# A Mamba block between two ternary feed-forward layers: the convolution reads u from PSUM

## The chip, the cores and the metric

One core of a Trainium2 chip. The metric is the device time of one execution in microseconds; lower is better. PE is TensorE, DVE VectorE, ACT ScalarE, POOL GpSimd, and SP the engine whose queue issues most DMAs.

## What is computed

For x of 4096 rows and 1024 columns, all in float32:

```python
x = x + 0.5 * ffn(layernorm(x))      # weight 1024x1024 made ternary: clip(round(w / mean|w|)) * mean|w|, and a bias
x = x + mamba(layernorm(x))
x = x + 0.5 * ffn(layernorm(x))      # the same weight and bias

def mamba(x):                        # 1024 channels, 16 states a channel
    u, z = split(x @ W_in.T)
    u = silu(conv_b + sum(conv_w[:, k] * up[:, k:k+L] for k in range(4)))   # up: u with three rows of zeros in front
    dt_r, B, C = split(u @ W_xproj.T)                                       # 64, 16, 16 columns
    dt = softplus(dt_r @ W_dt.T + b_dt)
    h_t = exp(dt_t * A) * h_(t-1) + dt_t * B_t * u_t                        # for each channel and state
    y = sum over states of (h_t * C_t) + u * Dskip
    return (y * silu(z)) @ W_out.T
```

The convolution is along the sequence: each row needs the three rows in front of it.

## The kernel before

The sequence is cut into 16 chunks of T = 256 rows. u, dt and the states h lie with the channels on the partitions and time along the free dimension; x, z and y lie with time on the partitions. u of a chunk is eight blocks of 128 channels, four to a half.

**Stages of a chunk.** `front()`: the first feed-forward layer (`ffn`: statistics on ACT and POOL, normed rows on ACT at L412, transposes on PE at L428, a split into a high and a low part at L456 and L458, matmuls at L499, the residual on DVE at L479), a second normalisation with its transposes, of which ACT makes the tile xT (L599), and then u: eight blocks of eight matmuls, each of which moves 256 columns of xT (L628). A float32 matmul appears in the profile as two passes. After each block a stream `conv` is spawned. `gates()` makes z (L680, L694, L699). `steps()` makes B, C and dt (L645 to L725). The recurrence runs state by state for each half: ACT makes the decays (L916), POOL the inputs dt*u*B (L937), DVE scans (L969) and multiplies by C (L984), some products are added in pairs on DVE (L999), and PE transposes and sums them in PSUM (L1022). `back()`: the gate (L1039), transposes (L755), W_out (L763), the residual on DVE (L734), the last feed-forward layer, and the output.

**The convolution before.** Two blocks share one PSUM bank: block j of a pair lies in columns j*256 and on. `conv` copies the last three columns of the chunk in front from the tile halo into the tile up (POOL, L556), copies the block from PSUM into up (ACT, L558), has POOL copy up's last three columns to halo for the next chunk (L548), makes the bias and the newest tap from PSUM (ACT, L561), and adds the three older taps one after the other on DVE, both tensor inputs in SBUF (L573):

```python
end = yield act(T, at)
nc.scalar.copy(up[:, KER - 1 :], rows_)
...
    nc.vector.scalar_tensor_tensor(ub, up[:, k : k + T], tap, ub, ALU.mult, ALU.add)
```

The bank is given back once ACT has read the pair's second block. After four blocks ACT applies silu to the half (L580).

**What sets the order.** The instructions of each engine run in the order in which they are issued, and a planner written into the kernel (the class `Streams`) chooses that order while the program is built. Each stage is a generator, a stream, with a rank; before an instruction it yields the engine, an assumed duration, the earliest time, and whether it needs the port that DVE and POOL share. The planner always issues the instruction that can start first by these assumptions, ties by rank; `HOLD` lets an engine wait some time for a stream of better rank. Constants are assumed costs and delays: `REACH` from one engine to another, `ISSUE` and `ADDED` for the DMA that adds the bias to x (L472, issued by POOL), `LATE_*` extra delays, and `DECAY`, `ENTER`, ..., `FFN_C`, `Z` the ranks. All of this only sets the order; on the chip semaphores decide when each instruction starts.

**Buffers.** PSUM has eight banks: three in the pool `banks` (u, z, out, feed-forward, transposes and dt take turns there), three for the decays, two for y. SBUF has five weight tiles of 512 KB, shared by the tiles of W_in for u, those for z, and those of W_out; `streamed()` keeps up to `ahead` tiles of one kind asked for. SP issues these loads (L364 u, L371 z, L377 W_out), and between them 512 broadcasts of B and C from DRAM (L886), x and the output.

Of the kernel before, what the change touches and what calls it, by code (L numbers as in the profile page):

```python
# [35 lines left out]
ALU = mybir.AluOpType  # L36
# [5 lines left out]
NST = 16  # L42
RANK = 64
KER = 4
EPS_LN = 1e-5
EPS_W = 1e-10

# [3 lines left out]

FULL, PASS, TURN = 0.844, 0.455, 0.855
REACH = 160
ISSUE, ADDED = 950, 9000
SWITCH = 1300

LATE_P, LATE_D, LATE_E, LATE_N = 300, 300, 300, 300
PAIRED = range(0, 4, 2)

DECAY, ENTER, SUM, PREPARE, RECUR, GATE = 4, 2, 1, 0, 5, 4  # L60
FFN_A, NORM, U_PART, CONV, DELTA, OUT, FFN_C = 0, 2, 3, 1, 0, 2, 3

HOLD = 100, 0, 250, 100
Z = 1, 4


class Streams:
# [109 lines left out]
def macaron_mamba_kernel(  # L177
# [34 lines left out]
    decays = buffers(3, [P, 2, T], "da", pool_=psum)  # L212
    ys = buffers(TT, [P, OH], "y", pool_=psum)
    xs = buffers(7, [P, D], "x")
    xts = buffers(2, [P, NB, T], "xT")
    his = buffers(2, [P, NB, P], "hi", F32R)
    los = buffers(2, [P, NB, P], "lo", F32R)
    weights = buffers(5, [P, D], "weight")
# [1 line left out]
    szs = buffers(2, [P, TT, OH], "sz")  # L220
    dts = buffers(2, [P, HB, T], "dt")
    tmps = buffers(2, [P, D], "tmp")
    ups = buffers(3, [P, KER - 1 + T], "up")
    xds = buffers(2, [P, 2, T], "xd")
    lns = buffers(4, [P, 40], "ln")
    hs = buffers(3, [P, HB, T], "h")
# [215 lines left out]
    def ffn(c, which, rank, at, tiles=range(TT)):  # L442
        ln, rows_, at = yield from stats(c, at, tiles)
        key = which, c

        def split(t):

            xn, begin = yield from normed(c, ln, rows_, t, at)
            hi = yield from his.take()
            lo = yield from los.take()  # L450
            ends = []

            def cut(g, pt, at_):
                part_hi, part_lo = (flat(p_[:, 4 * g : 4 * g + 4, :]) for p_ in (hi, lo))
                end = yield act(512, at_)
                nc.scalar.copy(part_hi, pt)  # L456
                end = yield dve(640, end + REACH)
                nc.vector.tensor_tensor(part_lo, pt, part_hi, ALU.subtract)  # L458
                banks.put(pt, end)
                ends.append(end)  # L460
                if len(ends) == NB // 4:
                    ready["parts", key, t] = end + REACH + LATE_N
                    parts[t] = lo, hi

            order.spawn(biased(t, begin), rank)
            yield from transposed(xn, begin, cut, rank)

        def biased(t, at_):

            yield from when("hbias")  # L470
            end = yield pool(ISSUE, at_, False)
            nc.gpsimd.dma_start(x_tiles[c, t], hbias.to_broadcast([P, D]), accum_op=ALU.add)  # L472
            ready["bias", key, t] = end + ADDED

        def residual(t, cols, pf, at_):
            at_ = max(at_, (yield from when("bias", key, t)))
            end = yield dve(650, at_)
            xt = x_tiles[c, t][:, cols]
            nc.vector.scalar_tensor_tensor(xt, pf, hscl, xt, ALU.mult, ALU.add)  # L479
            (ys if (*key, t) == ("a", 0, 1) else banks).put(pf, end)  # L480
            ready["ffn", key, t, cols.start] = end
            if key == ("c", NC - 1):
                yield from give_out(c, t, cols, end)

        parts = {}
        for t in tiles:
            order.spawn(split(t), rank)
        if key == ("a", 0):
            yield from as_weights_come(key, parts, residual, rank)
        for t in tiles if key != ("a", 0) else ():  # L490
            begin = yield from when("parts", key, t)
            lo, hi = parts[t]
            for h in range(2):
                cols = slice(h * OH, (h + 1) * OH)
                pf = yield from banks.take()
                for x in (lo, hi):
                    end = yield pe(8 * OH * PASS, 0, "r")
                    for k in range(NB):
                        nc.tensor.matmul(  # L499
                            pf,  # L500
                            x[:, k, :],
                            wf[:, k, cols],
                            start=(x is lo and k == 0),
                            stop=(x is hi and k == NB - 1),
                        )
                order.spawn(residual(t, cols, pf, end + REACH), rank)
            los.put(lo, end)
            his.put(hi, end)
        lns.put(ln, end if key != ("a", 0) else order.now)
        ends = {}  # L510
        for t in tiles:
            left = yield from when("ffn", key, t, 0)
            right = yield from when("ffn", key, t, OH)
            ends[t] = max(left, right)
        return ends
# [27 lines left out]
    u, sz, dt, xd, bc_dram, over = {}, {}, {}, {}, {}, {}  # L543


    def hand_over(c, blk, up, at):
        end = yield pool(140, at)
        nc.gpsimd.tensor_copy(halo[:, blk, :], up[:, T:])  # L548
        ready["halo", c, blk] = end

    def conv(c, blk, pp, at):
        half, b = divmod(blk, HB)
        up = yield from ups.take()
        ub, rows_ = u[c, half][:, b, :], pp[:, blk % 2, :]
        yield pool(140)
        nc.gpsimd.tensor_copy(up[:, 0 : KER - 1], halo[:, blk, :])  # L556
        end = yield act(T, at)
        nc.scalar.copy(up[:, KER - 1 :], rows_)  # L558
        order.spawn(hand_over(c, blk, up, end + REACH), CONV)
        end = yield act(T)  # L560
        nc.scalar.activation(  # L561
            ub,
            rows_,
            AF.Identity,
            bias=pr[:, blk, C_CB : C_CB + 1],
            scale=pr[:, blk, C_CW + KER - 1 : C_CW + KER],
        )
        if blk % 2:
            banks.put(flat(pp), end)
        for k in range(KER - 1):  # L570
            end = yield dve(405, end + (REACH if k == 0 else 115), True)
            tap = pr[:, blk, C_CW + k : C_CW + k + 1]
            nc.vector.scalar_tensor_tensor(ub, up[:, k : k + T], tap, ub, ALU.mult, ALU.add)  # L573
        end = max(end, (yield from when("halo", c, blk)))
        ups.put(up, end)
        done = ready.setdefault(("conv", c, half), [])
        done.append(end)
        if len(done) == HB:
            end = yield act(D, end + REACH, "silu")
            nc.scalar.activation(flat(u[c, half]), flat(u[c, half]), AF.Silu)  # L580
            ready["u", c, half] = end + REACH

    def front():
        for c in range(NC):
# [5 lines left out]
                at[t] = order.now + 5000  # L590
            ends = yield from ffn(c, "a", FFN_A, at)
            yield NORM
            queue = streamed(u_weights, NB, 2, U_PART)
            ln, rows_, at = yield from stats(c, ends)
            xT = yield from xts.take()

            def keep(g, pt, at_):
                end = yield act(512, at_)
                nc.scalar.copy(  # L599
                    xT[:, 4 * g : 4 * g + 4, t * P : (t + 1) * P],  # L600
                    pt.rearrange("p (j q) -> p j q", q=P),
                )
                banks.put(pt, end)
# [7 lines left out]
            for t in range(TT):  # L611
                xn, at = xns[t]
                yield from transposed(xn, at, keep, NORM)
                while len(ends) < 2 * (t + 1):
                    yield lambda: ends[2 * t + 1] if len(ends) > 2 * t + 1 else INF
            yield U_PART
            for pair in range(NB // 2):
                if 2 * pair % HB == 0:
                    u[c, 2 * pair // HB] = yield from us.take()
                pp = yield from banks.take()  # L620
                pp = pp.rearrange("p (j t) -> p j t", t=T)
                for j in range(2):
                    w = yield from arrived(queue)
                    wt = w.rearrange("p (k m) -> p k m", m=P)
                    for k in range(NB):
                        if k % 4 == 0:
                            end = yield pe(8 * T * FULL)
                        nc.tensor.matmul(  # L628
                            pp[:, j, :], wt[:, k, :], xT[:, k, :], start=(k == 0), stop=(k == NB - 1)
                        )  # L630
                    order.spawn(conv(c, 2 * pair + j, pp, end + REACH), CONV)
                    weights.put(w, end)
            order.spawn(gates(c, xT), Z[0])
            order.spawn(steps(c), DELTA)

# [26 lines left out]
        xds.put(xd[c], order.now + 2000)  # L662

    def gates(c, xT):
        queue = streamed(z_weights, NB, 3, Z[0])
        for half in range(2):
            yield Z[half]
            sz[c, half] = yield from szs.take()
            for b in range(0, HB, 2):
                pp = yield from banks.take()  # L670
                pp = pp.rearrange("p (t j) -> p t j", t=TT)
                for part_ in range(2):
                    w = yield from arrived(queue)
                    wt = w.rearrange("p (j k m) -> p j k m", j=2, m=P)
                    for t in range(TT):
                        end = yield pe(8 * T * FULL)
                        for i in range(HB):
# [1 line left out]

                            nc.tensor.matmul(  # L680
                                pp[:, t, :],
                                xT[:, k, t * P : (t + 1) * P],
                                wt[:, :, i, :],
                                start=(k == 0 and t == 0),
                                stop=(k == NB - 1),
# [91 lines left out]
    def back():  # L777
        for c in range(NC - 1):
            yield OUT
            queue = streamed(lambda i, w: out_weights(i // 2, i % 2, w), NB, 2, OUT)  # L780
            yT = []
            for half in range(2):
                yT.append((yield from us.take()))
                yield from turned(c, half, yT[half])
            for q in range(D // QW):
# [6 lines left out]
                        by_w_out(po, yT[half], w, half, t)  # L792
                    weights.put(w, end)
                for t in range(TT):
                    order.spawn(mixed(c, q, t, po, end + REACH), OUT)
            for half in range(2):
                us.put(yT[half], end)
            for q in range(D // QW):
# [324 lines left out]
```

## Time and profile before

| | |
|---|---|
| median of 3 runs | 2696.09 us (2694.91 to 2696.83) |
| the profiled execution | 2698.07 us, of which the span of the instructions is 2696.3 |
| granted TensorE clock, mean | 0.977 |
| HBM | 151 GB/s over the span |
| chain that ended last, shares | PE 35%, DVE 27%, ACT 15%, issue 12% |

The profile is of one execution. A group of instructions is named by its line, its engine, its operation and its tiles (out<-in); "busy" is the union of its instructions' times and "mean ns" the mean of one. Idle time ahead of a group is put down to the instruction whose semaphore came last. PE's ends are modelled: a pass of 256 columns is shown as 379 ns, while the next starts 216 ns after it. PEld is the load of the weights, which lies beside the matmuls.

### The profile page before, as it was taken

The page shows a single profiled execution, that of the slowest core. Times are in us where ns is not written, and L with a number is a line of the kernel's source. Part 1 is how long each engine was busy: PE and PEld are TensorE (multiplying, and loading weights), DVE is VectorE, ACT ScalarE, POOL GpSimd, SP SyncE. Part 2 cuts the span into 40 slices and gives each one's busy share as a digit, 9 for nine tenths or more (in the row PEclk, how much of TensorE's full clock was granted, in tenths as well). Part 3 has the DMA queues.
Part 4 walks back from the last instruction along what each step waited for, and adds up shares of the span by engine and source line. Part 5 has one row for each costly group of instructions (what it writes and reads, how often), then busy time and mean ns, then how long its engine had stood idle before and what let it go on. Part 6 is the DMA issues. An engine that isn't in the chain of part 4 may idle for free.

```text
span 2696.3 us, 40026 instructions
## 1 busy us (share of the span) xinstructions
PE 2522.3 (94%) x13570; PEld 2150.7 (80%) x13570; DVE 2436.7 (90%) x2500; ACT 2012.7 (75%) x4214; POOL 1802.3 (67%) x1657
## 2 busy tenths in 40 slices
PE   5988899999999999999999999999999999999887
PEld 4776788888888888888888888888888888888676
DVE  4588999999998999989999998999999899999894
ACT  3678688696877869687786878879687786967663
POOL 0356767677676776767677675767767577676773
PEclk8998899999999999999999999999999999999888
DMA  5443445645544555545555644554554456445451
GB/s 164 140 153 99 134 144 168 180 145 164 168 144 147 164 180 153 157 154 153 160 157 162 183 145 131 174 173 143 172 169 145 136 176 182 144 161 149 129 152 40
DMA packets 218550, 410.77 MB, mean 152 GB/s; under 512 B 19172, under 2 KB 85860, under 8 KB 218344
## 3 DMA queue, kind: packets, MB, share of 16 engines
q1 hardware_dynamic: 209128, 374.65, 42.3%
q0 software_dynamic: 9216, 33.56, 6.8%
q8 instruction: 107, 1.75, 0.3%
q14 instruction: 99, 0.81, 0.1%
HBM read 390.82 MB, written 17.31 MB: 151 GB/s over the span
## 4 chain that ended last, share of the span: by engine, by line
PE 35%; DVE 27%; ACT 15%; issue 12%; POOL 2%; DMA 2%; DVEq 0%; SPq 0%; POOLq 0%; ACTq 0%
DVE h L969 14%; PE bank L628 11%; DVE p L984 9%; PE bank L499 7%; PE bank L680 6%; ACT da L916 4%; PE y L1022 4%; PE bank L645 2%; PE bank L763 2%; DVE p L999 2%; PE bank L428 2%; ACT u L561 1%; DVE x L734 1%; POOL h L937 1%; ACT L916 1%
## 5 line engine op out<-in xcount | busy, mean ns | idle before, releaser
L937 POOL TENSOR_TENSOR h<-u,bc 128x1024 f32<-128x1024 f32 x512 | 1226.2, 2395 | 517.7 <-ACT da L916 212.0
L969 DVE TENSOR_TENSOR_SCAN h<-da,h 128x512 f32<-128x512 f32 x1024 | 1212.0, 1205 | 53.9 <-ACT da L916 42.2
L916 ACT ACTIVATE da<-dt,pr 128x255 f32<-128x255 f32 x2048 | 945.9, 474 | 89.2 <-DVE h L969 59.1
L984 DVE TENSOR_TENSOR p<-h,bc 128x1024 f32<-128x1024 f32 x512 | 684.8, 1338 | 0.1
L1022 PE MATMUL y<-ident,p 128*128 128x128 f32 x3840 | 513.5, 279 | 72.9 <-DVE p L984 65.0
L1022 PEld LDWEIGHTS y<-ident,p 128*128 128x128 f32 x3840 | 450.1, 144 | 139.7 <-DVE p L984 92.1
L628 PE MATMUL bank<-xT,weight 128*128 128x256 f32 x2048 | 472.8, 384 | 43.7 <-ACT u L561 32.2
L680 PE MATMUL bank<-weight,xT 128*128 128x256 f32 x2048 | 478.0, 381 | 0.0
L628 PEld LDWEIGHTS bank<-xT,weight 128*128 128x128 f32 x2048 | 380.5, 191 | 114.9 <-ACT u L561 53.4
L763 PE MATMUL bank<-weight,u 128*128 128x256 f32 x2016 | 465.4, 380 | 0.1
L680 PEld LDWEIGHTS bank<-weight,xT 128*128 128x128 f32 x2048 | 378.4, 191 | 46.1 <-issue 1.0
L763 PEld LDWEIGHTS bank<-weight,u 128*128 128x128 f32 x2016 | 371.5, 191 | 46.4 <-ACT da L916 1.8
L944 POOL TENSOR_TENSOR h<-h,over 128x4 f32<-128x4 f32 x512 | 285.4, 557 | 27.6 <-issue 0.3
L952 ACT COPY state<-h 128x4 f32<-128x4 f32 x512 | 98.8, 193 | 270.4 <-DVE h L969 269.7
L573 DVE SCALAR_TENSOR_TENSOR u<-up,pr,u 128x256 f32<-128x256 f32 x384 | 214.5, 591 | 95.4 <-ACT u L561 92.4
L499 PE MATMUL bank<-wf,lo 128*128 128x512 f32 x976 | 255.9, 404 | 4.2 <-DVE lo L458 3.7
L499 PE MATMUL bank<-wf,hi 128*128 128x512 f32 x976 | 247.5, 396 | 0.0
L499 PEld LDWEIGHTS bank<-wf,lo 128*128 128x128 f32 x976 | 180.6, 190 | 47.3 <-DVE lo L458 5.4
L499 PEld LDWEIGHTS bank<-wf,hi 128*128 128x128 f32 x976 | 182.5, 189 | 38.4
L548 POOL COPY halo<-up 128x3 f32<-128x3 f32 x128 | 45.7, 357 | 165.1 <-ACT up L558 164.9
L428 PE MATMUL bank<-ident,tmp 128*128 128x128 f32 x756 | 116.0, 285 | 32.0 <-ACT tmp L412 21.9
L558 ACT COPY up<-bank 128x256 f32<-128x256 f32 x128 | 47.0, 367 | 121.5 <-PE bank L628 119.1
(99 smaller groups left out, 2232.5 us busy)
## 6 DMA issues: line engine op xcount, KB each, us to landing
bc<-bcd SPq DMA_DIRECT2D x512, 256.0 KB, 3.7
weight<-in_w_out SPq DMA_DIRECT2D x128, 512.0 KB, 4.8
weight<-in_w_in SPq DMA_DIRECT2D x128, 512.0 KB, 3.7
weight<-in_w_in SPq DMA_DIRECT2D x256, 256.0 KB, 5.9
x<-hbias POOLq DMA_DIRECT2D x64, 512.0 KB, 8.2
x<-in_x SPq DMA_DIRECT2D x32, 512.0 KB, 5.2
out<-x SPq DMA_DIRECT2D x30, 512.0 KB, 4.5
weight<-in_w_ffn SPq DMA_DIRECT2D x5, 512.0 KB, 7.4
```

What stands on the lines that cost most here:

```text
L428: nc.tensor.matmul(pt[:, j * P : (j + 1) * P], xn[:, k * P : (k + 1) * P], ident, start=(j == 0), stop=(j == 3), is_transpose=True, skip_g ...
L499: nc.tensor.matmul(pf, x[:, k, :], wf[:, k, cols], start=(x is lo and k == 0), stop=(x is hi and k == NB - 1),)
L573: nc.vector.scalar_tensor_tensor(ub, up[:, k : k + T], tap, ub, ALU.mult, ALU.add)
L628: nc.tensor.matmul(pp[:, j, :], wt[:, k, :], xT[:, k, :], start=(k == 0), stop=(k == NB - 1))
L680: nc.tensor.matmul(pp[:, t, :], xT[:, k, t * P : (t + 1) * P], wt[:, :, i, :], start=(k == 0 and t == 0), stop=(k == NB - 1), skip_group_c ...
L763: nc.tensor.matmul(po[:, t, :], yT[:, b, t * P : (t + 1) * P], wt[:, b, :], start=(half == 0 and t == 0 and b == 0), stop=(half == 1 and b ...
L916: nc.scalar.activation(da[:, i, 1:], dt[c, half][:, b, 1:], AF.Exp, scale=a_neg[:, half * HB + b, n : n + 1],)
L937: nc.gpsimd.tensor_tensor(h, u[c, half], bc[:, 0:1, :].to_broadcast([P, HB, T]), ALU.mult)
L944: nc.gpsimd.tensor_tensor(h[:, :, 0], h[:, :, 0], over[c, half][:, :, n], ALU.add)
L969: nc.vector.tensor_tensor_scan(rows_, flat(da), rows_, 0.0, ALU.mult, ALU.add)
L984: nc.vector.tensor_tensor(p, h, bc[:, 1:2, :].to_broadcast([P, HB, T]), ALU.mult)
L1022: nc.tensor.matmul(y[t][:, b * P : (b + 1) * P], p[:, b, t * P : (t + 1) * P], ident, start=(first and b == 0), stop=(n == NST - 1 and b = ...
```

## The change

The convolution reads u where the matmuls leave it. A block now has a bank of its own, and its matmuls move 259 columns: the three of the chunk in front, whose u is computed a second time, and the 256 of this one. For that xT has four more columns in front (`PAD`), and halo holds three columns of xT instead of u: POOL copies them in ahead of a chunk's u matmuls and saves the new ones after the first block, two copies a chunk instead of sixteen. The tile up, ACT's copy into it, and the POOL copies for each block are gone. The taps on DVE have one input in PSUM, are reckoned at 335 instead of 405 ns, and are no longer planned as users of the shared port. The bank is given back after the third tap.

W_out's tiles are asked for once the product of state 12 of a chunk's second half is there, up to three ahead (before: at the chunk's start of `back()`, up to two). u's tiles are asked for up to four ahead (two), z's two (three). The residuals of the feed-forward layers and of W_out are planned 300 ns later (`LATE_X`), the bias DMA at 6000 instead of 9000 ns, and most ranks and one `HOLD` have other values.

```diff
-ISSUE, ADDED = 950, 9000
+ISSUE, ADDED = 950, 6000
-LATE_P, LATE_D, LATE_E, LATE_N = 300, 300, 300, 300
+LATE_P, LATE_X, LATE_D, LATE_E, LATE_N = 300, 300, 300, 300, 300
-DECAY, ENTER, SUM, PREPARE, RECUR, GATE = 4, 2, 1, 0, 5, 4
-FFN_A, NORM, U_PART, CONV, DELTA, OUT, FFN_C = 0, 2, 3, 1, 0, 2, 3
-HOLD = 100, 0, 250, 100
-Z = 1, 4
+DECAY, ENTER, SUM, PREPARE, RECUR, GATE = 5, 3, 1, 0, 5, 1
+FFN_A, NORM, U_PART, CONV, DELTA, OUT, FFN_C = 1, 0, 3, 2, 2, 2, 3
+HOLD = 100, 0, 250, 500
+Z = 2, 4
-    xts = buffers(2, [P, NB, T], "xT")
+    xts = buffers(2, [P, NB, PAD + T], "xT")
-    ups = buffers(3, [P, KER - 1 + T], "up")
...
     def conv(c, blk, pp, at):
         half, b = divmod(blk, HB)
-        up = yield from ups.take()
-        ub, rows_ = u[c, half][:, b, :], pp[:, blk % 2, :]
-        yield pool(140)
-        nc.gpsimd.tensor_copy(up[:, 0 : KER - 1], halo[:, blk, :])
+        ub, rows_ = u[c, half][:, b, :], pp[:, KER - 1 : KER - 1 + T]
         end = yield act(T, at)
-        nc.scalar.copy(up[:, KER - 1 :], rows_)
-        order.spawn(hand_over(c, blk, up, end + REACH), CONV)
-        end = yield act(T)
         nc.scalar.activation(
...
-        if blk % 2:
-            banks.put(flat(pp), end)
         for k in range(KER - 1):
-            end = yield dve(405, end + (REACH if k == 0 else 115), True)
+            end = yield dve(335, end + (REACH if k == 0 else 95))
             tap = pr[:, blk, C_CW + k : C_CW + k + 1]
-            nc.vector.scalar_tensor_tensor(ub, up[:, k : k + T], tap, ub, ALU.mult, ALU.add)
-        end = max(end, (yield from when("halo", c, blk)))
-        ups.put(up, end)
+            nc.vector.scalar_tensor_tensor(ub, pp[:, k : k + T], tap, ub, ALU.mult, ALU.add)
+        banks.put(pp, end)
...
-            queue = streamed(u_weights, NB, 2, U_PART)
+            queue = streamed(u_weights, NB, 4, U_PART)
...
+            end = yield pool(190)
+            nc.gpsimd.tensor_copy(xT[:, :, PAD - KER + 1 : PAD], halo)
+            at = max(end, ends[-1]) + REACH
             yield U_PART
-            for pair in range(NB // 2):
...
+            for blk in range(NB):
...
+                    nc.tensor.matmul(
+                        pp[:, : KER - 1 + T],
+                        wt[:, k, :],
+                        xT[:, k, PAD - KER + 1 : PAD + T],
+                        start=(k == 0),
+                        stop=(k == NB - 1),
+                    )
+                order.spawn(conv(c, blk, pp, end + REACH), CONV)
+                weights.put(w, end)
+                if blk == 0:
+                    yield pool(190, at)
+                    nc.gpsimd.tensor_copy(halo, xT[:, :, PAD + T - KER + 1 : PAD + T])
...
-        queue = streamed(z_weights, NB, 3, Z[0])
+        queue = streamed(z_weights, NB, 2, Z[0])
...
         for c in range(NC - 1):
             yield OUT
-            queue = streamed(lambda i, w: out_weights(i // 2, i % 2, w), NB, 2, OUT)
             yT = []
             for half in range(2):
+                if half:
+                    yield from when("product", c, 1, 12)
+                    queue = streamed(lambda i, w: out_weights(i // 2, i % 2, w), NB, 3, OUT)
```

In the changed kernel the lines of the parts spoken of are L550 (ACT's read of u), L560 (taps), L604 and L627 (POOL's two copies), L616 (u matmuls); the recurrence's and the later lines stand three to five lines further up than before (L966 scans, L981 products, L996 pair sums, L1019 y).

More of the change, by code (lines that the diff above doesn't have):

```diff
@@ L44 @@
 KER = 4
+PAD = 4
 EPS_LN = 1e-5
@@ L505, in ffn @@
                         )
-                order.spawn(residual(t, cols, pf, end + REACH), rank)
+                order.spawn(residual(t, cols, pf, end + REACH + LATE_X), rank)
             los.put(lo, end)
@@ L543, in macaron_mamba_kernel @@
     u, sz, dt, xd, bc_dram, over = {}, {}, {}, {}, {}, {}
[L546 to L549, printed above, removed]
     def conv(c, blk, pp, at):
         half, b = divmod(blk, HB)
-        up = yield from ups.take()
-        ub, rows_ = u[c, half][:, b, :], pp[:, blk % 2, :]
-        yield pool(140)
-        nc.gpsimd.tensor_copy(up[:, 0 : KER - 1], halo[:, blk, :])
+        ub, rows_ = u[c, half][:, b, :], pp[:, KER - 1 : KER - 1 + T]
         end = yield act(T, at)
-        nc.scalar.copy(up[:, KER - 1 :], rows_)
-        order.spawn(hand_over(c, blk, up, end + REACH), CONV)
-        end = yield act(T)
         nc.scalar.activation(
@@ L599, in keep @@
                 nc.scalar.copy(
-                    xT[:, 4 * g : 4 * g + 4, t * P : (t + 1) * P],
+                    xT[:, 4 * g : 4 * g + 4, PAD + t * P : PAD + (t + 1) * P],
                     pt.rearrange("p (j q) -> p j q", q=P),
@@ L615, in front @@
                     yield lambda: ends[2 * t + 1] if len(ends) > 2 * t + 1 else INF
+            end = yield pool(190)
+            nc.gpsimd.tensor_copy(xT[:, :, PAD - KER + 1 : PAD], halo)
+            at = max(end, ends[-1]) + REACH
             yield U_PART
-            for pair in range(NB // 2):
-                if 2 * pair % HB == 0:
-                    u[c, 2 * pair // HB] = yield from us.take()
+            for blk in range(NB):
+                if blk % HB == 0:
+                    u[c, blk // HB] = yield from us.take()
                 pp = yield from banks.take()
[L621 to L632, printed above, removed]
+                w = yield from arrived(queue)
+                wt = w.rearrange("p (k m) -> p k m", m=P)
+                for k in range(NB):
+                    if k % 4 == 0:
+                        end = yield pe(8 * (KER - 1 + T) * FULL, at)
+                    nc.tensor.matmul(
[10 more added lines that the diff above has]
+                    nc.gpsimd.tensor_copy(halo, xT[:, :, PAD + T - KER + 1 : PAD + T])
             order.spawn(gates(c, xT), Z[0])
@@ L681, in gates @@
                                 pp[:, t, :],
-                                xT[:, k, t * P : (t + 1) * P],
+                                xT[:, k, PAD + t * P : PAD + (t + 1) * P],
                                 wt[:, :, i, :],
@@ L794, in back @@
                 for t in range(TT):
-                    order.spawn(mixed(c, q, t, po, end + REACH), OUT)
+                    order.spawn(mixed(c, q, t, po, end + REACH + LATE_X), OUT)
             for half in range(2):
```

## The prediction

> **What bounds the kernel now.** I read, in this order: busy time by engine, the steady chunks cut out as stretches, the waits inside them, and then one wait as a timeline. Busy shares first:
>
> ```profile
> PE 2522.3 (94%) x13570; PEld 2150.7 (80%) x13570; DVE 2436.7 (90%) x2500; ACT 2012.7 (75%) x4214; POOL 1802.3 (67%) x1657
> ```
>
> PE is nearest to full, DVE next. A share over the span mixes the filling and draining of the pipeline with its middle, so I cut the middle at a place that returns in every chunk (the long run of u matmuls, at 828.58, 988.26, 1148.20 us and so on). Columns of a stretch: its length, then busy us (and instructions) of PE, PEld, DVE, ACT, POOL, the clock, DMA:
>
> ```profile
> 828.58:988.26 159.68, 155.07 (x849) 132.46 (x849) 150.88 (x154) 125.26 (x265) 112.07 (x103) 1.00 0.51 159
> 988.26:1148.20 159.94, 154.94 (x849) 132.44 (x849) 150.98 (x154) 125.27 (x265) 111.77 (x103) 1.00 0.52 158
> ```
>
> A chunk takes 159.7 us, with PE busy 155 (97%) at full clock. Busy DVE time flatters it: it includes waiting for the port that it shares with POOL (below). So PE's own order sets the chunk, and what can be won is PE's idle time and the slow restarts after it. The waits of the nine steady chunks (stretch 828 to 2265 us; us in total, times, longest) say where it idles:
>
> ```profile
> PEld bank L628 <- ACT u L561: 30.2, 36, 1.3
> PE bank L628 <- ACT u L561: 18.2, 27, 0.9
> PE y L1022 <- DVE p L984: 6.7, 15, 0.6
> PE bank L628 <- ACT up L558: 6.8, 9, 0.8
> PE bank L755 <- ACT da L916: 6.4, 9, 0.7
> ```
>
> The largest wait of PE is at L628, the u matmuls, for the convolution's two ACT reads of PSUM. PE and PEld tell of the same waits, so only PE is counted. The timeline of one (PE's lines, then ACT's; start, duration, in brackets the idle time before):
>
> ```profile
> 983.71 3.62 PE L628 MATMUL bank<-xT,weight 128*128 128x256 f32 x16
> 988.26 3.94 PE L628 MATMUL bank<-xT,weight 128*128 128x256 f32 x17 [0.93 <-ACT u L561]
> ```
> ```profile
> 987.37 0.37 ACT L558 COPY up<-bank 128x256 f32<-128x256 f32 x1 [1.36 <-PE bank L628]
> 987.63 0.57 ACT L561 ACTIVATE u<-bank,pr 128x256 f32<-128x256 f32 x1
> 988.09 0.26 ACT L872 ACTIVATE over<-over 128x64 f32<-128x64 f32 x1
> ```
>
> Two blocks share a bank. PE stops in the middle of the pair's second block, ACT reads the first block (987.37 to 988.20), and PE goes on at 988.26. The two engines take turns at one bank.
>
> **What goes.** The whole run's group row of L628 has 43.7 us of idle PE, 42.6 of it for L558 and L561 in 60 waits. Each wait costs more than its idle: the modelled end of a pass lies 0.16 us after the next pass's place (duration 0.379, pace 0.216), and the first pass after a wait takes 0.32 to the next start (988.257 to 988.577), 0.10 over the pace. So 0.26 a wait. In the nine steady chunks: 18.2 + 6.8 idle + 36 x 0.26 = 34.4 us, 3.8 a chunk. Three more chunks (337 to 828 us) have PE equally full (162 to 165 of 168 to 169 us): 11.5. Whole run 42.6 + 60 x 0.26 = 58.2, so 12.3 are left in the ends, where PE is 78 to 90% busy and other chains decide; I count a quarter, 3. **Gone: 49 us.**
>
> Also gone, beside the path: 128 ACT copies (47 us), 256 small POOL copies (55 + 46 us, 32 come back at some 0.5, the row of 128x64 at L868), and by the order of the built program ACT's table loads fall from 193 to 160 (33 x 1.28 = 42 us). ACT and POOL are 75% and 67% busy, so I take nothing for these, and lose nothing if they come back.
>
> **What comes.** (1) Three more columns in 2048 passes: 0.216 / 256 x 3 = 2.5 ns each, **+5.2 us** on PE, nothing hides it. (2) The taps' source is PSUM instead of SBUF. No row shows this form, so from both sides:
>
> ```profile
> L573 DVE SCALAR_TENSOR_TENSOR u<-up,pr,u x384: 451/477/2596, 59.8 to 2451.9; 128x256 f32<-128x256 f32 x192
> L479 DVE SCALAR_TENSOR_TENSOR x<-bank,hscl,x x124: 716/737/752, 39.7 to 2683.2; 128x512 f32<-128x512 f32 x124
> L734 DVE TENSOR_TENSOR x<-bank,x x126: 389/407/425, 301.7 to 2668.9; 128x256 f32<-128x256 f32 x126
> ```
>
> Durations are minimum/median/maximum. L734 (half the work of the operation, same size, from PSUM) gives 407; L479 is the operation itself from PSUM at 512 columns, and 256 columns less are worth 265 (mean 672 at L1039 against 407 at L734), so 472. I take 472: no dearer than the 477 of now. But the rows from PSUM have no tail, while L573 reaches 2596 and has a mean of 591: with both inputs in SBUF it waits for POOL, as the products do (L984, 1189/1215/2368). So DVE gains (591 - 472) x 384 = 46 us (71 at the other end), 2.9 a chunk, all on an engine that isn't the bound. It can only shorten what PE waits for from DVE (L1022, 6.7 us in nine chunks with 15 restarts, 1.2 a chunk): between 0 and all of it, I take 0.2 a chunk, **-3.5 us**.
>
> [...]
>
> (3) **The new wait.** A bank is now free after ACT's read and the third tap, and DVE's queue decides when. I worked this through by hand for one steady chunk of the new order. There z keeps one bank, so the eight u blocks alternate between two. With 3.5 us a block, 1.73 for half a z tile, 0.87 for eight y transposes, PE needs the bank of blocks 0 to 5 back, and wx needs that of block 6, 6.1, 6.1, 3.5, 4.4, 5.2, 6.9 and 5.2 us after the block's end. The release costs ACT 0.57 plus 0.2 of handing over, then three taps at 0.39 (their pace now), 1.9 in all, plus what stands between the taps in DVE's order: scans at 1.13, products at 1.14 to 1.3, pair sums at 1.14 to 1.96. Adding DVE's order up from block 0, the releases come 3.0, 0.7, 1.5 us early, then 0 to 0.6 late, 0.7 early to 0 late, 1.1 early to 0.2 late, and for wx 0.2 to 1.6 late. That is 0.2 to 2.4 a chunk; I take 0.8, x 16 = **+12.8 us** (3 to 38).
>
> (4) The halo's two copies a chunk on POOL: the first gates the u matmuls. In the order, out-projection and y groups of some 25 rows lie on PE between the last transposes and the first u block, which hides it; without that cover a POOL product in front costs 2.4 us a chunk. Behind the second stands the next product; POOL has 47 us a chunk free. (5) W_out's 128 issues go late in SP's queue, between the broadcasts of B and C, u's tiles are asked for four ahead. SP has nothing else to do (0.33 us an issue). With two buffers alternating, a W_out tile has 5.2 us from the last reader to the next; issued singly they landed in 3.5 to 4.0 (933 to 951 us of the trace), issued next to each other in 6.0 to 6.3. In the new order they stand singly: 0, and up to 1.1 x 4 a chunk if they bunch. (6) The bias DMA is reckoned at 6 us instead of 9, and lands after 8.2 (median). In the new order DVE's first residual stands 8.0 (after scan) and 5.8 us (before it) behind the first lo, and that 1.1 and 3.2 behind the issue: 9 us, so 0; if it lands 1 us late, 32 us on DVE. (7) The new ranks reorder everything else; its cost can't be read from the rows, I take 0, bounds of 38 us to both sides (the waits at L1022, L755 and at the transposes of the normed rows together make 2.7 a chunk).
>
> **Sum.** -49 + 5.2 - 3.5 + 12.8 = -34.5. The profiled execution took 2698.07 (span 2696.3 and 1.8 around it), the median of the runs is 2696.09, 2.0 less. 2698.1 - 34.5 - 2.0 = 2661.6, say **2661**, 1.3% faster; own range 2640 to 2685. A difference under 0.2% (5 us) can't be told from none.
>
> **Rivals.** *DVE holds the banks (slower).* Without (3) the change brings 47 us (49 + 3.5 - 5.2). If half of the 128 blocks find one more scan (1.13 us) ahead of their last tap, that is 72 us of PE waits, +25: 2721. It decides from 0.37 us of wait a block. For it: slack of at most 0.7 us at five of eight blocks, and any wait of DVE in that phase is now PE's; against it: DVE's work from PSUM has no tail. *The freed time is lost elsewhere (no change).* DVE's work of that phase, 36.3 us by the rows, equals PE's 36.7, so PE may just wait at y instead: 2692 to 2701. *The new order closes other waits too.* Half to all of the 2.7 a chunk, x 14: 19 to 38 better, 2623 to 2642. For it: ACT loses 89 us of work and DVE 46. *Late weights or bias (it doesn't do what it says).* By (5), 4.4 a chunk x 16 = 70 more: about 2731.
>
> **How the numbers follow.** Forecast 0.50, order better still 0.20, no change 0.09, banks held 0.17, late DMAs 0.04. Faster by over 0.2%: 0.70; within: 0.09; slower: 0.21. From 2620 to 2712 there lies all but the worse part of the slow cases and a little below.
>
> **What would show it.** Right: no wait of L616 (u) for ACT; waits of L616 for DVE L560 under 1.5 us a chunk; L560 at 0.41 to 0.48 without a tail; u passes at a pace of 0.219; steady chunk near 157 us. Wrong: PE waiting over 3 us a chunk for L560, L560's mean over 0.55, PE waiting for DMA at L758, or DVE waiting for a DMA at L479.

## The result, and the profile after

The changed kernel took 2673.02 us (median of 5 runs, 2668.41 to 2674.70), the kernel before 2696.29 in the same series: ratio 0.991, interval 0.9896 to 0.9925. That is 23.3 us less, where 35 were forecast. Busy time by engine after:

```profile
PE 2512.2 (94%) x13570; PEld 2146.8 (80%) x13570; DVE 2353.0 (88%) x2500; ACT 1931.9 (72%) x4054; POOL 1688.0 (63%) x1433
```

ACT, DVE and POOL are busy 81, 84 and 114 us less, PE nearly as much as before (10 us less), and the time falls by much less than any of the three gained. Two steady chunks after, cut at the first u matmul (length, busy PE, PEld, DVE, ACT, POOL, clock, DMA):

```profile
805.40:964.20 158.80, 153.85 (x849) 132.25 (x848) 144.68 (x154) 119.92 (x254) 105.05 (x89) 1.00 0.52 160
964.20:1123.00 158.80, 154.24 (x850) 132.21 (x849) 144.90 (x156) 120.29 (x254) 104.98 (x89) 1.00 0.52 160
```

The middle has hardly moved. From the first u matmul of the fifth chunk to that of the fifteenth, ten chunks took 1596.4 us before and 1592.0 after: 0.4 a chunk. Of the 23.4 us that the span lost, 6.6 lie in front of that, 4.4 in it and 12.4 behind it. So the place where most of the gain was forecast brought a fifth of it. The waits of PE in the nine steady chunks after (805 to 2238 us) say why:

```profile
PE bank L616 <- DMA weight<-in_w_in: 17.1, 9, 2.5
...
PE bank L428 <- ACT tmp L412: 7.8, 9, 0.9
...
PE bank L675 <- DMA weight<-in_w_in: 6.7, 7, 1.1
...
PE bank L499 <- DVE lo L458: 4.8, 9, 0.5
PE bank L499 <- ACT dt L720: 3.2, 9, 0.4
```

In these chunks PE's u matmuls wait neither for ACT nor for a tap. They wait for their own weights instead, which no wait of PE in the trace before did. One such wait, on the timeline:

```profile
1136.33 0.96 POOL L472 DMA_DIRECT2D x<-hbias  x1 [1.41 <-ACT tmp L412]
...
1137.17 4.09 SPq L364 DMA_DIRECT2D weight<-in_w_in  x2
1139.34 1.19 POOL L472 DMA_DIRECT2D x<-hbias  x1
...
1147.81 3.51 PE L616 MATMUL bank<-xT,weight 128*128 128x259 f32 x15 [2.53 <-DMA weight<-in_w_in]
```

Two bias DMAs go out at 1136 and 1139, two u tiles are asked for from 1137.17 on, and PE stands still until 1147.8. The landing of u's tiles shows it for the run (minimum, median, maximum; before they were 3.3, 3.7 and 5.8):

```profile
DMA to landing us min/median/max: 3.3/5.2/10.3
```

From 640 us on, the trace has the landing of 72 u tiles. 27 of them were under way beside a bias DMA and took 8.2 us in the median, the other 45 took 4.5. In the kernel before none was beside one.

### The profile page after: what moved, and what is told of

The parts are those of the page before. It is cut to its first block, busy times and chain, and to the rows that moved or that the text cites. A ratio compares the mean times of both kernels' runs of the same rounds, so it can differ in the third digit from the quotient of the medians.

```text
span 2672.9 us, 39584 instructions
## 1 busy us (share of the span) xinstructions
PE 2512.2 (94%) x13570; PEld 2146.8 (80%) x13570; DVE 2353.0 (88%) x2500; ACT 1931.9 (72%) x4054; POOL 1688.0 (63%) x1433
## 5 line engine op out<-in xcount | busy, mean ns | idle before, releaser
L966 DVE TENSOR_TENSOR_SCAN h<-da,h 128x512 f32<-128x512 f32 x1024 | 1221.0, 1209 | 135.3 <-ACT da L913 105.4
L981 DVE TENSOR_TENSOR p<-h,bc 128x1024 f32<-128x1024 f32 x512 | 668.8, 1306 | 0.1
L1019 PE MATMUL y<-ident,p 128*128 128x128 f32 x3840 | 512.7, 278 | 49.0 <-DVE p L981 43.8
L1019 PEld LDWEIGHTS y<-ident,p 128*128 128x128 f32 x3840 | 454.7, 144 | 111.2 <-DVE p L981 62.4
L616 PE MATMUL bank<-xT,weight 128*128 128x259 f32 x2048 | 478.0, 387 | 25.9 <-DMA weight<-in_w_in 22.2
L675 PE MATMUL bank<-weight,xT 128*128 128x256 f32 x2048 | 480.1, 382 | 13.8 <-DMA weight<-in_w_in 10.3
L616 PEld LDWEIGHTS bank<-xT,weight 128*128 128x128 f32 x2048 | 385.4, 192 | 90.6 <-issue 24.8
L941 POOL TENSOR_TENSOR h<-h,over 128x4 f32<-128x4 f32 x512 | 245.8, 480 | 32.1
L560 DVE SCALAR_TENSOR_TENSOR u<-bank,pr,u 128x256 f32<-128x256 f32 x384 | 180.4, 471 | 49.6 <-ACT u L550 46.3
L499 PEld LDWEIGHTS bank<-wf,hi 128*128 128x128 f32 x976 | 179.8, 189 | 43.5 <-issue 4.0
L395 POOL TENSOR_SCALAR ln<-ln 128x1 f32<-128x1 f32 x96 | 63.0, 656 | 177.3 <-ACT tmp L393 174.9
L550 ACT ACTIVATE u<-bank,pr 128x256 f32<-128x256 f32 x128 | 71.6, 559 | 125.8 <-PE bank L616 125.8
L393 ACT ACTIVATE tmp<-x 128x1024 f32<-128x1024 f32 x96 | 100.7, 1049 | 77.0 <-DMA x<-in_x 34.6
```

The costliest lines, as they stand in the source:

```text
L393: nc.scalar.activation(xn[t], x_tiles[c, t], AF.Identity, accum_out=sums[:, t : t + 1])
L499: nc.tensor.matmul(pf, x[:, k, :], wf[:, k, cols], start=(x is lo and k == 0), stop=(x is hi and k == NB - 1),)
L560: nc.vector.scalar_tensor_tensor(ub, pp[:, k : k + T], tap, ub, ALU.mult, ALU.add)
L616: nc.tensor.matmul(pp[:, : KER - 1 + T], wt[:, k, :], xT[:, k, PAD - KER + 1 : PAD + T], start=(k == 0), stop=(k == NB - 1),)
L675: nc.tensor.matmul(pp[:, t, :], xT[:, k, PAD + t * P : PAD + (t + 1) * P], wt[:, :, i, :], start=(k == 0 and t == 0), stop=(k == NB - 1), ...
L941: nc.gpsimd.tensor_tensor(h[:, :, 0], h[:, :, 0], over[c, half][:, :, n], ALU.add)
```

## The experiments

All times are medians, with the kernel before at 2696.6 to 2697.2 beside them on the same chips. "A chunk" is the mean of the ten in the middle, cut as above.

**1. Each half of the change alone.** `conv_only` is the changed kernel with the old numbers:

```diff
-ISSUE, ADDED = 950, 6000
+ISSUE, ADDED = 950, 9000
-DECAY, ENTER, SUM, PREPARE, RECUR, GATE = 5, 3, 1, 0, 5, 1
+DECAY, ENTER, SUM, PREPARE, RECUR, GATE = 4, 2, 1, 0, 5, 4
...
-                    queue = streamed(lambda i, w: out_weights(i // 2, i % 2, w), NB, 3, OUT)
+            queue = streamed(lambda i, w: out_weights(i // 2, i % 2, w), NB, 2, OUT)
```

> The changed kernel's convolution (taps from PSUM, a bank for each block, 259 columns) with the old ranks, HOLD, LATE_X 0, ADDED 9000 and the old times of asking for weights. Theory (the turns at one bank were the cost): PE's waits of the u matmuls for ACT fall from 43 us to under 5, and the time to 2655 to 2685. Rival 1 (the gain is the new order's): within 10 us of 2696, or slower, because DVE holds the banks in an order that was not chosen for it.

Measured: 2720.6, ratio 1.009 (1.0075 to 1.0105), 163.6 a chunk. u hardly waits for ACT's read any more (0.6 us in one wait), as the theory said, but the time went the other way, as rival 1 had it. `order_only` is the reverse: the new numbers on the old convolution.

> The kernel before, its convolution untouched, with the new ranks, HOLD, LATE_X, ADDED 6000 and the new times of asking for weights. Theory: 2685 to 2720, since two blocks still share a bank and PE still waits some 40 us for ACT's reads. Rival 1: 2665 to 2680, most of the gain without the convolution's edit.

Measured: 2876.6, ratio 1.0669 (1.0653 to 1.0685), 171.4 a chunk. Neither half alone is faster, and the time lies above both ranges. Rival 1 falls, and so does the simple form of the theory: the same new numbers took 48 us off the direct read and cost the old convolution 180.

**2. The turns at the bank, alone.** `own_bank` is the kernel before with a bank for each u block, and nothing else: ACT still copies u to SBUF, the taps still read the copy.

```diff
-        ub, rows_ = u[c, half][:, b, :], pp[:, blk % 2, :]
+        ub, rows_ = u[c, half][:, b, :], pp[:, :T]
...
-        if blk % 2:
-            banks.put(flat(pp), end)
+        banks.put(pp, end)
...
-                pp = yield from banks.take()
-                pp = pp.rearrange("p (j t) -> p j t", t=T)
                 for j in range(2):
+                    pp = yield from banks.take()
```

> The kernel before with one edit: each u block takes a bank of its own, ACT's copy to up and the taps from SBUF stay, the bank is given back after ACT's two reads. Theory: it is the turns of PE and ACT at a shared bank that cost, so PE's waits for L558 and L561 go and the time falls by 20 to 45 us, to 2650 to 2676, without any tap from PSUM. Rival 2 (it was the work taken from ACT, POOL and DVE's port that brought the gain): within 8 us of 2696.

Measured: 2626.0, ratio 0.9737 (0.9723 to 0.9752), 155.2 a chunk. This beats both kernels, by more than expected. Its u matmuls over the whole run (minimum, median, maximum duration, then all that they waited for), where before there were 43.7 us of idle time:

```profile
L626 PE MATMUL bank<-xT,weight x2048: 379/379/796, 52.9 to 2373.5; 128*128 128x256 f32 x187
...
its engine sat idle before it (us, times) until:
  ACT xT L598: 0.2, 1
```

And PE's waits in nine steady chunks (790 to 2187 us):

```profile
PE y L1020 <- DVE p L982: 8.0, 19, 0.6
PE bank L753 <- ACT da L914: 6.4, 9, 0.7
...
PE bank L428 <- DVE lo L458: 2.7, 9, 0.3
```

These are the other waits of the kernel before, nearly unchanged (6.7, 6.4 and 2.7 there). What went is the turns and only them, and ACT, POOL and DVE do the same work as before: rival 2 falls.

A better order isn't what made it faster either. The planner came to the same order: in the two traces the instructions of PE, DVE, ACT, POOL and SP follow one another in exactly the same sequence (by operation, tiles and shapes) over the whole program. So the 71 us are the price of the shared bank at a fixed order. By the profiled executions 44 us of it lie in the ten middle chunks, 18 in front of them and 10 behind.

**3. The bias DMA beside the u tiles.** Two kernels keep the changed kernel's order on PE, DVE, ACT and SP, and on POOL too but for the bias DMA, which they let go later:

```diff
+            if which == "c" and 1 < c < NC - 2:
+                yield lambda: end + 18000
             nc.gpsimd.dma_start(x_tiles[c, t], hbias.to_broadcast([P, D]), accum_op=ALU.add)
```

The first of them moved the wrong one, that of the first layer (`which == "a" and c > 2`):

> The changed kernel, same order on PE, DVE, ACT and SP; from the fourth chunk on POOL issues the bias DMA of the first feed-forward layer 18 us later, after the u tiles have landed (its sum is needed some 40 us after the old issue). Theory: u's tiles land late (5.3 us in the median against 3.7 before) because this DMA now runs beside them; L616's waits for DMA fall from 22 us to under 6 and the time by 15 to 25 us. Rival: the tiles are late because their buffer is free late; waits and time within 5 us of the changed kernel.

Measured: 2755.2, ratio 1.0207 (1.0178 to 1.0236). The waits of the u matmuls for weights stayed (18.5 us), and DVE now waited for the sum, which in that layer is needed some 10 us after the old issue (the expectation's 40 us are the other layer's):

```profile
DVE x L481 <- DMA x<-hbias: 52.1, 13, 7.3
```

With that 52 us of wait in DVE's queue, where the scans stand behind it, the time rose to 82 us above the changed kernel's. It says nothing of the collision. The second moved the right one:

> The bias DMA that runs beside the u tiles was the other layer's: in the changed kernel the last feed-forward layer's is issued in the u phase, 42 us before its sum is needed. Here that one goes 18 us later on POOL from the third chunk on, the order of PE, DVE, ACT and SP as in the changed kernel. Theory: L616's waits for DMA fall from 22 us to under 6, and the time by 12 to 25 us from 2673. Rival (the tiles' buffers are free late): within 5 us of 2673, waits stay.

Measured: 2659.0, ratio 0.986 (0.9845 to 0.9875), 157.9 a chunk instead of 159.2. The u matmuls' wait for weights is gone from the steady chunks (805 to 2227 us). The wait for weights that is left there is z's; it stands first here, with two others:

```profile
PE bank L677 <- DMA weight<-in_w_in: 7.7, 7, 2.2
...
PE bank L428 <- ACT tmp L412: 6.7, 8, 0.9
PE bank L501 <- DVE lo L458: 6.1, 9, 0.7
```

The collision is shown: 14 us, with all other queues in the same order, and the u tiles' median landing down from 5.2 to 4.3 us (3.7 in the kernel before). Tile by tile, the 27 that took 8.2 us beside a bias DMA took 4.2 here, the other 45 about 4.5 in both. The rival (a buffer that is free late) falls for u.

**4. What the direct read costs.** `own_bank` beats the changed kernel by 47 us, so I looked for the price of the hold and of the 259 columns. `own_bank_hold` gives the bank back after the third tap:

```diff
-        banks.put(pp, end)
         for k in range(KER - 1):
...
+        banks.put(pp, end)
         end = max(end, (yield from when("halo", c, blk)))
```

> own_bank (2626) with one edit: the bank is given back after the third tap, though the taps read the copy in SBUF. Theory (the hold until DVE's third tap is what costs the direct read its gain): a chunk goes from 155.2 to 158 or more, the time to 2665 to 2730. Rival 3 (the 259 columns, the taps from PSUM or halo's copies cost it): within 15 us of 2626.

Measured: 2722.6, ratio 1.0101 (1.0084 to 1.0117), chunks of 158.6 to 172, inside the theory's range. `copy_259` puts the copy back into `conv_only`:

```diff
+        nc.scalar.copy(up, pp[:, : KER - 1 + T])
...
+        banks.put(pp, end)
         for k in range(KER - 1):
...
-            nc.vector.scalar_tensor_tensor(ub, pp[:, k : k + T], tap, ub, ALU.mult, ALU.add)
-        banks.put(pp, end)
+            nc.vector.scalar_tensor_tensor(ub, up[:, k : k + T], tap, ub, ALU.mult, ALU.add)
```

> conv_only (2721) with the copy put back: 259 columns are computed, ACT copies all of them to a tile in SBUF, the taps read it, and the bank is given back after ACT's two reads; halo holds columns of xT, so POOL's copies for each block stay away. Old ranks and asks. Theory: the hold was the cost, so 2620 to 2650, at 155.2 + 0.3 a chunk or a little better than own_bank since POOL has less to do. Rival 3: 2690 or more.

Measured: 2695.9, ratio 0.9992 (0.9982 to 1.0001). 25 us under `conv_only`, but 70 over `own_bank`, which by the numbers speaks for rival 3. Its chunks run from 155.3 to 169.9, though, and PE's largest wait in them is that of transposes for normed rows (26.7 us in 6 waits in nine chunks, none in the nine of `own_bank`), which neither the columns nor halo touch. And `own_bank_new`, the new numbers on `own_bank`:

> own_bank with the new ranks, HOLD, LATE_X, ADDED and asks. Theory: these values were fitted to the direct read; with a copy they are no better than the old ones, 2626 to 2800 (the same values cost 180 us on the kernel before). Rival 1 (the new order is better by itself): under 2615.

Measured: 2823.7, ratio 1.0469 (1.0453 to 1.0485). That is 24 us above the theory's range and far from rival 1's.

**5. Is it the order?** PE's order of a chunk repeats exactly in the steady chunks of the kernel before, the changed kernel and `own_bank`, and doesn't in `conv_only`, `copy_259` and `own_bank_hold`. A fourth theory was that this costs. One number brings a repeating order:

```diff
-HOLD = 100, 0, 250, 100
+HOLD = 100, 150, 250, 100
```

(in `own_bank_hold_s` 500 instead of 150).

> Control. own_bank with HOLD for DVE at 150 instead of 0, so the planner's order moves while the design stays. In own_bank PE's order repeats from chunk to chunk, in the kernel before and the changed one too; in conv_only, copy_259 and own_bank_hold it doesn't, and their chunks took 155 to 172 us. Theory 4 (part of those kernels' loss is an order that wanders, not their design): 2615 to 2645 here, since this order repeats as well. If the planner's luck alone made own_bank fast: 2665 or more.

> copy_259 (2696) with the same HOLD of 150, with which PE's order repeats. Theory 4: 2625 to 2645, which is own_bank's 155.2 and 0.3 for the three columns in a chunk. Rival 3 (259 columns or halo's new copies cost it): 2685 or more.

> conv_only (2721) with the same HOLD of 150, with which PE's order repeats; the bank is held until the third tap. Theory (the hold costs, beside what the wandering order costs): 2660 to 2690, 2.5 to 4 us a chunk over copy_259_s. If the hold costs nothing once the order repeats: 2620 to 2645.

> own_bank_hold (2723) with HOLD for DVE at 500, with which PE's order repeats; taps from SBUF, the bank given back after the third. Theory: 2660 to 2690. If the hold costs nothing once the order repeats: 2620 to 2645.

Measured: 2835.8 (ratio 1.0517, 1.0501 to 1.0533), 2724.3 (1.0103, 1.0088 to 1.0118), 2712.7 (1.0064, 1.0048 to 1.0081) and 2811.2 (1.0428, 1.0413 to 1.0444). Of the ranges only the open ones ("or more") were met. The fourth theory falls: the control, `own_bank`'s design in an order that repeats as well, is 210 us slower than `own_bank`. Its waits over the run:

```profile
PEld bank L428 <- ACT tmp L412: 196.7, 43, 12.6
PE bank L428 <- ACT tmp L412: 184.0, 41, 12.6
PEld y L1020 <- DVE p L982: 86.8, 75, 10.0
PE y L1020 <- DVE p L982: 65.2, 37, 9.8
```

The order alone moves one design by more than either half of the change moved the kernel before; the 210 us came with a lower granted clock as well (0.949 over the profiled execution, 0.979 in `own_bank`'s). By the control's expectation such a time would mean that luck alone made `own_bank` fast. It was lucky to keep a good order, but that order is the kernel before's, so their difference is not luck. The times of group 4, each with an order of its own, can't be read as prices of the hold or the columns. What a bank held until the third tap costs in time stays open. As a wait that PE shows for a tap it is small: none in the changed kernel and in the two kernels that keep the copy and hold the bank, 5.0 us in `conv_only`, 8.5 in `conv_only_s`. What is not open is what was seen at a fixed order: the shared bank (group 2) and the collision (group 3).

## Why the prediction was right, and where its sum was not

The accounts of PE in eight steady chunks, from each pass's start to the next one's, in us a chunk:

| | before | after | bias_later_c | own_bank |
|---|---|---|---|---|
| u | 30.1 | 30.3 | 28.6 | 27.7 |
| z | 28.4 | 29.1 | 29.0 | 28.3 |
| y | 29.7 | 27.4 | 27.8 | 27.9 |
| feed-forward | 30.2 | 31.2 | 31.2 | 30.2 |
| transposes of normed rows | 5.5 | 5.9 | 6.1 | 5.5 |
| all of the chunk | 159.7 | 158.9 | 157.8 | 155.2 |

(A wait of u that begins behind a y group counts under y.)

**What goes: right in kind, too small in size.** The turns cost 3.8 a chunk by the prediction; `own_bank` saves 4.5 at the same order, of which u and y, where the turns lie, are 4.1. The trace shows PE stopped within a block for a read of other columns of the same bank (0.93 us idle until 988.26, with ACT's reads from 987.37 to 988.20), and with a bank for each block the idle time ahead of the u matmuls fell from 43.7 us to 0.2. Why the turns are taken by bank and not by columns, no run shows. The whole run was reckoned at 49 us, a quarter of the waits in the ends; `own_bank` saved 71 with every queue in the same order, 28 of it outside the ten middle chunks, where some 11 had been counted. One cause is in the reading "PE and PEld tell of the same waits, so only PE is counted". The page's row of the weight loads has more:

```profile
L628 PEld LDWEIGHTS bank<-xT,weight 128*128 128x128 f32 x2048 | 380.5, 191 | 114.9 <-ACT u L561 53.4 <-ACT up L558 14.2 <-ACT xT L599 0.2
```

That is 67.6 us in 78 waits, where PE's row has 42.6 in 60. In the ten middle chunks PEld's waits for ACT make 43.5 us, and `own_bank` saved 44.4 there.

**The three columns: right.** u's pace went from 216 to 218 ns a pass; 5 us.

**The taps from PSUM: right.** Their group after:

```profile
L560 DVE SCALAR_TENSOR_TENSOR u<-bank,pr,u x384: 449/476/486, 57.3 to 2441.0; 128x256 f32<-128x256 f32 x192
```

476 where 472 were taken, and the tail to 2596 is gone: the mean fell from 591 to 471, 46 us of DVE as a sum of durations, as worked out (34 as the union of their times). In the median a tap from PSUM cost DVE what one from SBUF had cost: 476 ns against 477. What the prediction and the planner call the shared port is in the traces as a wait: before, 64 of the 384 taps took more than 486 ns, and each of these had a POOL instruction beside it; the 170 with none beside them took 486 at most. After, 280 had one beside them and none took more than 486.

**The new wait for DVE: none.** 12.8 us were taken, and no wait of L616 for L560 appears in the trace. By hand I had some releases late, by up to 0.6 us for u and 1.6 for wx; the trace shows none. That doesn't show the hold to be free: the planner had spread other work around it.

**Steps (5) and (7), taken at nothing: this is where the sum failed.** Step (5) looked at the tiles of W_out and at SP's queue, found both free, and didn't ask what else would be moving data when u's tiles land. The new ranks, step (7), norm the last feed-forward layer's rows in the u phase, and with that the bias DMA goes out there, 42 us before its sum is needed (`order_only`, with the new numbers and the old convolution, has 25 of 74 u tiles beside one as well). u and z waited 24 us for weights in nine chunks where nothing waited before, 2.6 a chunk without the restarts; the collision with u alone is worth 14 us of time. Step (6) looked at the same DMA, but only for DVE that waits for its sum, not for what it slows. The feed-forward matmuls lost another 1.0 a chunk to new waits for lo and dt.

**DVE's relief: more than was priced, and not told apart from the new order.** It was priced at 0.2 a chunk, 3.5 for the whole run. PE's wait at y for products, which the prediction showed at 6.7 us in nine steady chunks, is nearly gone after:

```profile
PE y L1019 <- DVE p L981: 0.7, 3, 0.3
```

Behind the fifteenth chunk's first u matmul it fell from 27.6 us to 15.5. `own_bank`, with DVE's work unchanged, kept both (8.0 and 29.6). Whether the lighter taps or the new order brought it, no run tells apart, nor what share it has in the 12.4 us won at the end, since the turns went there too. The 6.6 us in front weren't looked into.

**The signs.** Four of five came: no wait of u for ACT in the steady chunks, none for a tap, L560 at 0.47, u's pace at 0.218. The fifth, a steady chunk near 157 us, didn't: 159.2. (ACT's table loads, beside the path, fell to 161 and not to 160.)

So the forecast was faster, and it is faster, by 23 of 35 us, and that the two lie so near is in part luck: the turns were taken too small and 12.8 us were charged for a wait that didn't come, while the new waits for weights, lo and dt weren't on the list at all. The rival of late weights or bias named the right kind of thing at the wrong tiles.

## What to carry to other kernels

Two blocks in one PSUM bank made the matmuls and the reading engine take turns here; a bank for each, with nothing else changed, the order of every queue included, was worth 2.6%, more than the larger rewrite. When an order is planned anew, look at what each transfer will now run beside, above all transfers that are needed late and issued early. And a change that is tried with a planner can't be judged by its time alone: compare waits, and see whether the order of the queues stayed the same.

## What the runs showed of the hardware that wasn't expected

Beside a DMA issued by POOL that adds a broadcast row to 512 KB in SBUF, the landing of a 512 KB load took nearly twice as long here (8.2 us in the median and up to 10.3, against 4.2 for the same 27 loads without it). The mean DMA share of a steady chunk, 0.52, hides this: in the stretch of the timeline above, the 16 DMA engines of the core are full by this view, with a share of 1.02 (length, busy PE, PEld, DVE, ACT, POOL, clock, DMA share, GB/s):

```profile
1140.00:1148.00 8.00, 5.47 (x30) 4.53 (x29) 8.00 (x10) 4.50 (x7) 3.70 (x5) 1.00 1.02 267
```

In six other stretches of 7.5 to 10 us with such a pair the share was 0.98 to 1.04.

Of the other thing, that the taps of 256 columns with two inputs cost DVE the same with one of them in PSUM (476 ns) as with both in SBUF (477) and that only the second form has a tail (up to 2596 ns against 486), the rows had told half.
